# Reordering the first group of batches of an attention kernel: norms in a row, a later bias addition, alternating PSUM banks

## The chip, the cores and the metric

The kernel runs on one core of a Trainium2 chip. A time is the device time of one whole execution in microseconds (us). All executions told of here are of the state "fast" (the usual, undisturbed one) unless said otherwise. A ratio is the mean time of one kernel's fast runs over the mean of the other's fast runs of the same rounds on the same chip, so it is not quite the ratio of the medians that I quote. An interval behind a ratio is its 95% interval.

Engines in the profile: PE is TensorE's matmul stream, PEld its weight load, DVE VectorE, ACT ScalarE, POOL GpSimd, SP SyncE. "PEclk" is the granted TensorE clock as a share of full speed. A pass is one matmul record of the profile; a float32 product shows as two (the adjacency product of one batch is x2 at L306 of the kernel before), a transpose as one (four are x4 at L299). PSUM is the memory of the tiles that the kernel's matmuls write; a bank is one half of its two-bank tiles.

## The reference

128 batches `x[b]` of 128 x 512 float32 go through two pre-norm layers. Cut to what matters:

```python
h = max(layernorm(x), 0)
C = adj @ h + b;  x = x + max_over_nodes(relu(C))    # one number per row (A - A cancels)
# layer 1
h = max(layernorm(x), 0)
q, k, v = h @ Wq + bq, h @ Wk + bk, h @ Wv + bv       # 8 heads of 64
w = softmax(q k^T / 8 + mask(adj == 0))
out = x + w v
```

The first layer adds one number to a whole row, and the second norm takes a row's mean away, so one norm serves both. The weights of a softmax sum to 1, so `bv` may be added to `x` itself, once, at any time before the output. That freedom is what the change uses.

## The kernel before

Batches are worked in groups of four. The first two groups and two batches of the third are prepared by a hand-written beginning; then a loop over 128 batches takes a batch's scores, mask, weighted sum and output, and in the gaps the projections of the next group and the norm of the batch ten ahead. The parts that matter:

```python
def norm_end(m):
    nc.vector.tensor_scalar(HN[m], X[g][:, i, :], MV[m][:, 0:1], 0.0, op0=ALU.subtract, op1=ALU.max)
    nc.scalar.activation(HN[m], HN[m], AF.Copy, scale=RSTD[m])
    nc.gpsimd.tensor_tensor(X[g][:, i, :], X[g][:, i, :], bv_sb, op=ALU.add)
# norm(m), before it: statistics on VectorE, rstd on GpSimd (a power)

def transposes(m):                       # "Tm" in what follows
    ph = ps_sc.tile([P, 2, NC, D], F32, name="sc")       # pool of one two-bank tile
    for c in range(NC):
        nc.tensor.transpose(ph[:, 0, c], HN[m][:, c * P : (c + 1) * P], ident)
    nc.scalar.copy(HT[g][:, i], ph[:, 0])

def adjacency(m, pa=None):               # "Am"
    nc.tensor.matmul(pa, adjT, HN[m], start=True, stop=True)
    nc.vector.reduce_max(AMAX[g][:, i : i + 1], pa, axis=AX.X)

for m in range(G):
    norm(m); norm_end(m)
    if m > 0:
        early(m - 1)                     # early(m): transposes(m), adjacency(m)
plain_q(0)                               # 2 banks, each written and read by halves
early(G - 1)
...                                      # k and v products of group 0, early(4) ... A9
# ---- the loop, at its end:
    if m < B:
        adjacency(m)
    finish(g, i, w)                      # weighted sum, output
```

## Time and profile before

| | before |
|---|---|
| median (range), 3 runs | 1621.87 us (1621.35 to 1623.84) |
| span of the profiled execution | 1620.0 us |
| TensorE busy | 98% |
| first scores of the loop | 75.04 us |
| batch 124's scores, where the last group begins | 1594.57 us |
| from there to the end of the flag (the last VectorE instruction), "the tail" | 22.63 us |
| from there to the end of the span, "the exit" | 2.79 us |

I split the span at three marks, because TensorE bounds most of it: the first scores, the scores of batch 124 (the first of the last four, after which no projections are left to fill the gaps), and the flag that the kernel computes last. The marks are read from the chain of waits; the timeline has the same scores start 0.06 to 0.07 us earlier.

The tail in the kernel before, from the timeline (start, duration, engine, line, what, and the idle time before):

```profile
1600.54 1.16 PE L477 MATMUL sc<-qT,kT 64*128 64x128 f32 x16
1603.22 0.34 PE L499 MATMUL pav<-v,w 128*64 128x65 f32 x4 [1.52 <-DVE w L490]
...
1604.70 1.16 PE L477 MATMUL sc<-qT,kT 64*128 64x128 f32 x16
```

The reader sees a period of 4.16 us: scores, 1.5 us of waiting for the mask, the weighted sum, scores again. TensorE idles here, because nothing is left to put in.

### The profile page before, as it was taken

The page shows a single profiled execution, that of the slowest core. Times are in us where ns is not written, and L with a number is a line of the kernel's source. Part 1 is how long each engine was busy: PE and PEld are TensorE (multiplying, and loading weights), DVE is VectorE, ACT ScalarE, POOL GpSimd, SP SyncE. Part 2 cuts the span into 40 slices and gives each one's busy share as a digit, 9 for nine tenths or more (in the row PEclk, how much of TensorE's full clock was granted, in tenths as well). Part 3 has the DMA queues.
Part 4 walks back from the last instruction along what each step waited for, and adds up shares of the span by engine and source line. Part 5 has one row for each costly group of instructions (what it writes and reads, how often), then busy time and mean ns, then how long its engine had stood idle before and what let it go on. Part 6 is the DMA issues. An engine that isn't in the chain of part 4 may idle for free.

```text
span 1620.0 us, 29469 instructions
## 1 busy us (share of the span) xinstructions
PE 1586.6 (98%) x11819; PEld 1319.8 (81%) x11819; DVE 1114.2 (69%) x2044; ACT 422.9 (26%) x844; POOL 259.6 (16%) x278
## 2 busy tenths in 40 slices
PE   6899999999999999999999999999999999999996
PEld 4688888888888888888888888888888888888885
DVE  3576777766777767777767777667777677777655
ACT  2322222222222222222222222222222222222221
POOL 4311111111111111111111111111111111111000
PEclk9999999999999999999999999999999999999999
DMA  4033222232222232222332222322222322223201
GB/s 164 1 72 73 68 60 51 69 75 69 63 46 70 69 79 65 67 44 69 72 73 68 54 56 69 76 68 64 47 69 69 79 65 67 44 69 73 47 27 40
DMA packets 299082, 104.02 MB, mean 64 GB/s; under 512 B 264448, under 2 KB 264576, under 8 KB 298944
## 3 DMA queue, kind: packets, MB, share of 16 engines
q1 hardware_dynamic: 297520, 99.69, 25.5%
q8 instruction: 94, 1.54, 0.4%
q10 hardware_dynamic: 1248, 2.16, 0.4%
q14 instruction: 44, 0.36, 0.1%
q0 software_dynamic: 176, 0.27, 0.1%
HBM read 37.03 MB, written 33.55 MB: 44 GB/s over the span
## 4 chain that ended last, share of the span: by engine, by line
PE 97%; DVE 1%; ACT 1%; issue 0%; DMA 0%; POOL 0%; ACTq 0%; DVEq 0%; POOLq 0%
PE mm L372 72%; PE pav L499 9%; PE sc L477 8%; PE mm L306 6%; PE mm L445 1%; PE pav L306 1%; PE sc L299 0%; DVE w L490 0%; DMA xg<-in_x_dram 0%; ACT hn L272 0%; DVE o L512 0%; DVE o L508 0%; POOL rstd L264 0%; DVE st L259 0%; ACT qT L450 0%
## 5 line engine op out<-in xcount | busy, mean ns | idle before, releaser
L264 POOL TENSOR_TENSOR rstd<-ve,mhalf 128x1 f32<-128x1 f32 x128 | 84.3, 659 | 1225.9 <-DVE ve L262 1087.6
L485 ACT ACTIVATE w<-sc 128x512 f32<-128x512 f32 x256 | 138.9, 595 | 515.4 <-PE sc L477 515.4
L499 PEld LDWEIGHTS pav<-v,w 128*64 128x64 f32 x4096 | 130.3, 137 | 99.6 <-issue 54.4
L372 PE MATMUL mm<-hs,sq_sb 128*128 128x256 f32 x744 | 179.0, 383 | 0.0
L372 PE MATMUL mm<-hs,sk_sb 128*128 128x256 f32 x768 | 176.4, 379 | 0.0
L372 PE MATMUL mm<-sv_sb,hs 128*128 128x256 f32 x768 | 176.2, 379 | 0.0
L273 POOL TENSOR_TENSOR xg<-xg,bv_sb 128x512 f32<-128x512 f32 x128 | 162.9, 1273 | 35.2 <-DVE hn L269 27.5
L490 DVE TENSOR_TENSOR w<-w,live 128x512 f32<-128x512 f32 x256 | 164.7, 685 | 1.0 <-ACT w L485 1.0
L372 PEld LDWEIGHTS mm<-sv_sb,hs 128*128 128x128 f32 x768 | 145.9, 190 | 20.7 <-issue 1.0
L272 ACT ACTIVATE hn<-hn,rstd 128x512 f32<-128x512 f32 x128 | 92.9, 726 | 267.7 <-DVE hn L269 206.3
L372 PEld LDWEIGHTS mm<-hs,sk_sb 128*128 128x128 f32 x768 | 145.9, 190 | 20.3 <-issue 0.5
L372 PEld LDWEIGHTS mm<-hs,sq_sb 128*128 128x128 f32 x744 | 138.8, 190 | 21.4
L499 PE MATMUL pav<-v,w 128*64 128x65 f32 x4096 | 148.5, 224 | 6.7 <-DVE w L490 6.7
L477 PE MATMUL sc<-qT,kT 64*128 64x128 f32 x2048 | 148.7, 285 | 0.0
L420 DVE TENSOR_TENSOR u<-mm,p1b 128x512 f32<-128x512 f32 x63 | 43.5, 691 | 128.3 <-PE mm L372 128.3
L477 PEld LDWEIGHTS sc<-qT,kT 64*128 64x128 f32 x2048 | 124.2, 187 | 9.1 <-issue 0.3
L372 PE MATMUL mm<-hT,wk_sb 128*128 128x256 f32 x512 | 124.2, 385 | 0.0
L372 PE MATMUL mm<-wv_sb,hT 128*128 128x256 f32 x512 | 120.9, 379 | 0.0
L306 PE MATMUL mm<-hn,adjT 128*128 128x512 f32 x236 | 120.5, 592 | 0.0
L372 PE MATMUL mm<-hT,wq_sb 128*128 128x256 f32 x496 | 120.4, 386 | 0.0
L372 PEld LDWEIGHTS mm<-wv_sb,hT 128*128 128x128 f32 x512 | 97.3, 190 | 13.7 <-issue 0.5
L372 PEld LDWEIGHTS mm<-hT,wk_sb 128*128 128x128 f32 x512 | 94.7, 190 | 15.8 <-issue 0.5
(84 smaller groups left out, 2033.1 us busy)
## 6 DMA issues: line engine op xcount, KB each, us to landing
out_dram<-o SPq DMA_DIRECT2D x128, 256.0 KB, 2.1
xg<-in_x_dram SPq DMA_DIRECT2D x62, 512.0 KB, 5.1
hT<-tb SPq DMA_DIRECT2D x960, 32.0 KB, 2.0
xg<-in_x_dram SPq DMA_DIRECT2D x2, 256.0 KB, 3.4
xg<-in_x_dram ACTq DMA_DIRECT2D x2, 256.0 KB, 5.6
wq_sb<-in_L_gnn_Wq_dram SPq DMA_DIRECT2D x1, 512.0 KB, 7.9
wk_sb<-in_L_gnn_Wk_dram SPq DMA_DIRECT2D x1, 512.0 KB, 11.1
wq_sb<-in_L_gnn_Wq_dram ACTq DMA_DIRECT2D x1, 512.0 KB, 10.6
```

The lines of the kernel that those rows point to most:

```text
L264: nc.gpsimd.tensor_tensor(rstd, ve, mhalf, op=ALU.pow)
L272: nc.scalar.activation(HN[m], HN[m], AF.Copy, scale=RSTD[m])
L273: nc.gpsimd.tensor_tensor(X[g][:, i, :], X[g][:, i, :], bv_sb, op=ALU.add)
L306: nc.tensor.matmul(pa, adjT, HN[m], start=True, stop=True)
L372: nc.tensor.matmul(bank[:, r, :], lhs, rhs, start=first and r == 0 and c == 0, stop=r == 1 and c == 1, skip_group_check=True,)
L420: nc.vector.tensor_tensor(self.u3, self.b, self.pf[1], op=ALU.add)
L445: nc.tensor.matmul(bank[:, r, :], W["q"][:, c, k * P : (k + 1) * P], h[:, :, c], start=r == 0 and c == 0, stop=r == 1 and c == NC - 1, ski ...
L477: nc.tensor.matmul(psc[:, j, f, :], KT[g][r, f, i * D : (i + 1) * D], QT[g][r, f, i * D : (i + 1) * D], start=True, stop=True,)
L485: nc.scalar.activation(w[:, j], psc[:, j], AF.Exp, scale=HD ** -0.5)
L490: nc.vector.tensor_tensor(w[:, j], w[:, j], live_h, op=ALU.mult)
L499: nc.tensor.matmul(pav[r, h // 4, (h % 4) * HE : (h % 4 + 1) * HE], w[:, h % 2, h // 2, r], V[g % 2][:, i, h, :], start=True, stop=True,)
```

## The change

Its intent: start TensorE earlier and leave fewer holes before the first scores. Four parts: (1) all four norms of the first group in a row, with four buffers; (2) the `bv` additions of these four moved to the loop; (3) transposes and adjacency products in the two halves (banks) of one PSUM tile in turn, and `plain_q` by whole banks, with adjacency products between; (4) the norm of a later batch begun right after the adjacency product of the one before. Besides these, ScalarE's activation table is loaded early by a dummy instruction (the load takes 1.28 us in both kernels, from 5.58 us before and from 5.65 us after), and some sums move. The core:

```diff
+        nc.gpsimd.memset(mhalf, -0.5)
+        nc.scalar.activation(live[:, 0:1], mhalf, AF.Copy)
         make_identity(nc, ident)
@@ norm_end
-            nc.gpsimd.tensor_tensor(X[g][:, i, :], X[g][:, i, :], bv_sb, op=ALU.add)
+            if m >= G:
+                add_bv(m)
@@ transposes (adjacency likewise, with ps_av)
-            ph = ps_sc.tile([P, 2, NC, D], F32, name="sc")
+            if i % 2 == 0:
+                PH[g] = ps_sc.tile([P, 2, NC, D], F32, name="sc")
+            ph = PH[g][:, i % 2]
@@ the beginning
             for m in range(G):
                 norm(m)
                 norm_end(m)
-                if m > 0:
-                    early(m - 1)
-            plain_q(0)
-            early(G - 1)
+            transposes(0)
+            transposes(1)
+            plain_q(0, 0)
+            for m in (2, 3):
+                transposes(m)
+            for m in (0, 1):
+                adjacency(m)
+            plain_q(0, 1)
+            for m in (2, 3):
+                adjacency(m)
 ... (sums and norms of the second group: cut)
-                if s >= 8 and s < 12:
-                    h_sum(1, s - 8)
+                if s in (7, 8, 9, 10):
+                    h_sum(1, s - 7)
@@ the loop
                 w = scores(g, i)
+                if g == 0:
+                    add_bv(b)
```

More of the change, by code (lines that the diff above doesn't have):

```diff
@@ L208, in fast @@
         ps_av = ctx.enter_context(tc.tile_pool(name="ps_av", bufs=1, space=PSUM))
-        X, HN, TB, HT, HB, QT, KT, C, AMAX, WA, RSTD, MV, PR = ({} for _ in range(13))
+        X, HN, TB, HT, HB, QT, KT, C, AMAX, WA, RSTD, MV, PR, PH, PA = ({} for _ in range(15))
         def load(g):
@@ L235, in fast @@
         load(2)
+        nc.gpsimd.memset(mhalf, -0.5)
+        nc.scalar.activation(live[:, 0:1], mhalf, AF.Copy)
         make_identity(nc, ident)
-        nc.gpsimd.memset(mhalf, -0.5)
         nc.gpsimd.memset(ones, 1.0)
@@ L245, in fast @@
         nc.scalar.copy(adjT, pt[:, :D])
-        nc.vector.tensor_single_scalar(live, adjT, 0.0, op=ALU.not_equal)
         live_h = live.unsqueeze(1).to_broadcast([P, NC, D])
@@ L255, in norm @@
                 C[g] = stat.tile([P, G], F32, name="c")
-            HN[m] = proj.tile([P, N], F32, name="hn")
+            if m in (2, 3):
+                if m == 2:
+                    TB[0] = proj.tile([P, NQ, 2, NC, Q], F32, name="tb")
+                HN[m] = TB[0].rearrange("p a i c r -> p (a i c r)")[:, (m - 2) * N : (m - 1) * N]
+            else:
+                HN[m] = proj.tile([P, N], F32, name="hn")
             st = stat.tile([P, 6], F32, name="st")
@@ L272, in norm_end, with add_bv @@
             nc.scalar.activation(HN[m], HN[m], AF.Copy, scale=RSTD[m])
-            nc.gpsimd.tensor_tensor(X[g][:, i, :], X[g][:, i, :], bv_sb, op=ALU.add)
+            if m >= G:
+                add_bv(m)
+        def add_bv(m):
+            x_m = X[m // G][:, m % G, :]
+            nc.gpsimd.tensor_tensor(x_m, x_m, bv_sb, op=ALU.add)
         def blocks(m):
@@ L296, in transposes, with adjacency @@
             g, i = divmod(m, G)
-            ph = ps_sc.tile([P, 2, NC, D], F32, name="sc")
+            if i % 2 == 0:
+                PH[g] = ps_sc.tile([P, 2, NC, D], F32, name="sc")
+            ph = PH[g][:, i % 2]
             for c in range(NC):
-                nc.tensor.transpose(ph[:, 0, c], HN[m][:, c * P : (c + 1) * P], ident)
-            nc.scalar.copy(HT[g][:, i], ph[:, 0])
-        def adjacency(m, pa=None):
+                nc.tensor.transpose(ph[:, c], HN[m][:, c * P : (c + 1) * P], ident)
+            nc.scalar.copy(HT[g][:, i], ph)
+        def adjacency(m):
             g, i = divmod(m, G)
-            if pa is None:
+            if m >= 2 * G + 2:
                 pa = ps_mm.tile([P, 512], F32, name="mm")
+            else:
+                if i % 2 == 0:
+                    PA[g] = ps_av.tile([P, 2, 512], F32, name="pav")
+                pa = PA[g][:, i % 2]
             nc.tensor.matmul(pa, adjT, HN[m], start=True, stop=True)
@@ L433, in p3, with plain_q @@
                 self.add(self.dst(0, 1), self.c, self.u2)
-        def plain_q(t):
-            if t == 0:
+        def plain_q(t, f):
+            if t == 0 and f == 0:
                 QT[0] = proj.tile([P, NC, T], F32, name="qT")
             h = HT[0][:, 2 * t : 2 * t + 2]
-            for f in range(2):
-                bank = ps_mm.tile([P, 2, HT2], F32, name="mm")
-                for r in range(2):
-                    k = 2 * f + r
-                    for c in range(NC):
-                        nc.tensor.matmul(
-                            bank[:, r, :], W["q"][:, c, k * P : (k + 1) * P], h[:, :, c],
-                            start=r == 0 and c == 0, stop=r == 1 and c == NC - 1,
-                            skip_group_check=True,
-                        )
-                    nc.scalar.activation(
-                        QT[0][:, k, t * HT2 : (t + 1) * HT2], bank[:, r], AF.Identity,
-                        bias=bq_sb[:, k : k + 1],
-                    )
+            bank = ps_mm.tile([P, 2, HT2], F32, name="mm")
+            for r in range(2):
+                for c in range(NC):
+                    nc.tensor.matmul(
+                        bank[:, r, :], W["q"][:, c, (2 * f + r) * P : (2 * f + r + 1) * P],
+                        h[:, :, c], start=r == 0 and c == 0, stop=r == 1 and c == NC - 1,
+                        skip_group_check=True,
+                    )
+            for r in range(2):
+                k = 2 * f + r
+                nc.scalar.activation(
+                    QT[0][:, k, t * HT2 : (t + 1) * HT2], bank[:, r], AF.Identity,
+                    bias=bq_sb[:, k : k + 1],
+                )
         def products(g):
@@ L517, in fast @@
         with tc.manual_schedule():
-            def early(m):
-                transposes(m)
-                adjacency(m, ps_av.tile([P, 2, 512], F32, name="pav")[:, 0])
             for m in range(G):
@@ L526, in fast @@
                 norm_end(m)
-                if m > 0:
-                    early(m - 1)
-            plain_q(0)
-            early(G - 1)
+            nc.vector.tensor_single_scalar(live, adjT, 0.0, op=ALU.not_equal)
+            transposes(0)
[8 more added lines that the diff above has]
+                adjacency(m)
             weight_sums(nc.vector, "k")
+            plain_q(1, 0)
+            weight_sums(nc.gpsimd, "v")
             for k in range(4):
                 h_sum(0, k)
-            plain_q(1)
-            weight_sums(nc.gpsimd, "v")
+            norm(G)
+            norm_end(G)
+            plain_q(1, 1)
             _, k, v = PR[0] = [None] + [Products(0, n) for n in "kv"]
+            m = G
             for s, p in enumerate((
@@ L540, in fast @@
                 p()
-                m = G + s // 2
-                if m < 2 * G + 2:
-                    if s % 2 == 0:
+                if s % 2 == 0 and m < 2 * G + 2:
+                    if m < 2 * G:
+                        transposes(m)
+                    else:
+                        blocks(m)
+                    adjacency(m)
+                    m += 1
+                    if m < 2 * G + 2:
                         norm(m)
                         norm_end(m)
-                    elif m < 2 * G:
-                        early(m)
-                    else:
-                        blocks(m)
-                        adjacency(m, ps_av.tile([P, 2, 512], F32, name="pav")[:, 0])
-                if s >= 4 and s % 2 == 0 and s < 12:
-                    weight_sum(nc.gpsimd, "q", s // 2 - 2)
-                if s >= 8 and s < 12:
-                    h_sum(1, s - 8)
+                if s in (2, 4, 6, 9):
+                    weight_sum(nc.gpsimd, "q", (2, 4, 6, 9).index(s))
+                if s in (7, 8, 9, 10):
+                    h_sum(1, s - 7)
             move(2 * G + 1)
```

## The prediction

> **What bounds the kernel now.** I read the page first, then the busy table by stretches, the chain of waits for the first 130 us, the timeline of that stretch, and the transfers' landing times.
>
> ```profile
> span 1620.0 us, 29469 instructions
> PE 1586.6 (98%) x11819; PEld 1319.8 (81%) x11819; DVE 1114.2 (69%) x2044; ACT 422.9 (26%) x844; POOL 259.6 (16%) x278
> PE   6899999999999999999999999999999999999996
> ```
>
> TensorE is busy 98% of the span. One digit of the last line is 40.5 us: only the first two or three slices and the last leave it idle, so the span is one TensorE stream of fixed length, and a change of the beginning can only move its start and the holes before it becomes solid. The stretches show the holes (columns: TensorE, weight load, VectorE, ScalarE, GpSimd):
>
> ```profile
> 10.00:15.00 5.00, 0.47 (x1) 0.00 (x0) 3.08 (x5) 0.91 (x2) 2.89 (x3) 1.00 1.05 386
> 15.00:20.00 5.00, 4.66 (x12) 2.74 (x13) 1.73 (x5) 1.53 (x3) 2.07 (x4) 1.00 1.05 387
> ...
> 50.00:55.00 5.00, 3.31 (x17) 2.59 (x17) 2.62 (x6) 0.77 (x2) 2.21 (x3) 1.00 0.00 0
> ```
>
> From 75.04 us, where the chain reaches the first scores, it holds nothing but TensorE through 130 us. So I ask only when the first scores start. The timeline tells why TensorE stands still from 10.5 to 15.3 us (columns: start, duration, engine, line, what):
>
> ```profile
> 12.11 1.26 POOL L273 TENSOR_TENSOR xg<-xg,bv_sb 128x512 f32<-128x512 f32 x1 [6.42 <-DVE mv L260]
> 12.12 1.53 DVE L269 TENSOR_SCALAR hn<-xg,mv 128x512 f32<-128x512 f32 x1
> 13.33 0.73 POOL L264 TENSOR_TENSOR rstd<-ve,mhalf 128x1 f32<-128x1 f32 x1
> ...
> 14.09 0.72 ACT L272 ACTIVATE hn<-hn,rstd 128x512 f32<-128x512 f32 x1 [6.35 <-POOL rstd L264]
> 14.72 0.57 ACT L300 COPY hT<-sc 128x512 f32<-128x512 f32 x1
> ...
> 15.34 1.11 PE L299 MATMUL sc<-ident,hn 128*128 128x128 f32 x4 [4.87 <-ACT hT L300]
> ```
>
> The 6.42 us before GpSimd's addition are put down to VectorE, which had long been done. The bv load, issued at 3.5 us, took 8.5 us to land by the table of transfers: 12.0 us. [...]the first batch's bv addition holds up the second batch's rstd (whose input was ready at 6.3 us), and so on through scaling, ScalarE's copy and the second transposes. Later holes:
>
> ```profile
> 22.51 3.72 PE L445 MATMUL mm<-hT,wq_sb 128*128 128x256 f32 x16 [0.56 <-ACT qT L450]
> ...
> 54.26 0.66 PE L299 MATMUL sc<-ident,hn 128*128 128x128 f32 x4 [1.69 <-ACT hn L272]
> ...
> 65.92 1.13 PE L306 MATMUL pav<-hn,adjT 128*128 128x512 f32 x2 [1.76 <-ACT hn L272]
> ...
> 72.19 1.12 PE L306 MATMUL pav<-hn,adjT 128*128 128x512 f32 x2 [1.69 <-ACT hn L272]
> ```
>
> Here the norm is begun only after the previous adjacency's maximum, with two projection products too few beside it; and inside the plain q projection half a bank waits four times for ScalarE to read the other half.
>
> [...]a pass of the adjacency product takes 0.86 us up to 18 us and 0.43 us at 29 us; the switch lies near 19.4 us, 4.1 us after work resumes at 15.34. [...]1.53 us above beside the bv addition, 0.48 us otherwise. [...]
>
> **The change part by part.** No arithmetic is removed; TensorE's matmuls are the same. I write Tm, Am for transposes and adjacency of batch m.
>
> *Table load.* ScalarE's own DMA issues run to 5.49 us (the last waits for x of batch 1), and before, the load started at 5.58. Worth 0.1 us, eaten by the dummy activation: 0.
>
> *Four norms in a row.* rstd of batch 1 is free at 7.1 us instead of 14.06. Batch 3's x is last: issued at 1.65, 7.3 us to landing (the median of that queue's two is 5.6, the first took 3.9), so about 8.95. From the trace's norm: statistics to rstd's end 1.9 us (3.77 to 5.70), so 10.9; scaling 0.7, so 11.6.
>
> *Alternating banks.* I read the waits of the built program, which was not run. T1 waits for ScalarE's copy of T0, T3 for that of T2, A1 for the maximum of A0, A2 of A1, A3 of A2: the guard is kept per tile, and both halves are one tile. So the second bank does not pay. Worse, ScalarE's first copy stands behind all four scalings. Chain: scaling 3 issued 10.93, next ScalarE instruction 0.63 later (as 14.09 to 14.72), copy 0 11.56 to 12.13, T1 12.18 to 13.29 (1.11 at half clock), copy 1 13.33 to 13.90, first q matmul 13.95. Both halves of wq have landed (2.16 plus 10.6 is 12.8).
>
> *TensorE's work from there to the first scores*, full clock, from the chain: 64 q passes and 13 products of 8 passes at 1.74 per 8: 13.9 and 22.6; T2 to T7 at 0.44: 2.6; A0 to A9 at 0.86: 8.6. Sum 47.7.
>
> *Losses after the change* (estimates from the trace's durations): half clock for about 4 us, 2.0. T3 behind copy 2, which stands behind two qT activations (0.84) and takes 0.57: 1.15. A1 and A3 behind a maximum of 0.69 plus 0.2: 0.9 each (A2 has a q half between). For T4 to T7 the chain maximum, statistics, rstd, scaling, measured as 3.5 us from A5's last pass issued (44.08) to the next transposes (47.60), stands beside two products of 3.47: 0.05 each. A8 0.2, A9 0.5, as VectorE has more queued there. Sum 5.9, and 0.7 for what I also cannot assign before (next line): 6.6. First scores: 13.95 + 47.7 + 6.6 = 68.25.
>
> *Check on before:* from T1 at 15.34 the work is 13.9 + 22.6 + 7 × 0.44 + 9 × 0.86 = 47.3; to 75.04 12.4 are lost. Half clock 2.0; four qT waits at 0.54 plus 0.26 of drain, 3.2; T4 0.7, T6 1.84, A8 1.91, A9 1.84, T5 and T7 0.15: 11.6, 0.7 not assigned. The method holds.
>
> Gain 75.04 − 68.25 = 6.8 us: start 15.34 to 13.95 with 0.4 more work left, 1.0; losses 12.4 to 6.6, 5.8. Of these the q order gives 3.2, the norms begun earlier and the maxima about 5.5, against 2.95 of new waits. The four bv additions (1.27 us each, GpSimd 16% busy) run beside the first group's scores: 0. The tail is untouched. 1621.9 − 6.8 = 1615.
>
> **Rivals.** (a) The banks do alternate, if the waits are released by halves: T1 right after scaling 1, q at 12.8, none of the 2.95: 4.1 us more, 1611. For it: the code's intent; against: the waits name those copies and maxima. (b) [...]a q half of 16 passes at 0.43 is 6.9 us, loss up to 3.4 instead of 2.0, and some more of the small holes: 1617. (c) The norms, squeezed just under two products, slip: each T4 to A9 loses 0.5 rather than 0.05, 1617 to 1618. (d) TensorE must run 1586 us anyway and the gain is absorbed by a transfer later: the chain after 75 us has no DMA piece, so I hold it unlikely; 1621.
>
> **Range and chances.** All rivals lie within 11 us of before, while 2% are 32 us. The size of the mis-reckoning I allow is the clock switch (±1.2), the tight norms (+1.5), the waits by tile (−2.9). 1615, 1612 to 1618 for eight in ten; faster by over 2% 0.01, within 98%, slower 0.01.
>
> **What would show it.** In the changed profile: first scores near 68 us; T1 near 12.2 us released by ScalarE's copy, not by the scaling of batch 1; first q matmul near 13.95; passes of 0.43 until about 18 us; no q matmul waiting for a qT activation; A1 and A3 idle near 0.9 after a maximum; T3 idle near 1.1; scaling of batch 3 at 10.9. It is wrong if T1 runs near 8.6 us, if T4 to A9 show holes over 0.5 us, or if the chain after the first scores has pieces that are not TensorE.

## The result, and the profile after

The changed kernel took 1619.07 us in the median (1618.37 to 1621.22, 4 runs), the kernel before 1621.74 us (1621.35 to 1623.84, 4 runs); the ratio is 0.9983 [0.9966, 1.0]. (The fourth run of the kernel before came with this result.) So 2.7 us were gained, not 6.8, and 1619.07 lies above the range of 1612 to 1618. By the interval of the ratio the gain lies anywhere between 0 and 5.5 us, and by the rule of 2% the two kernels are equally fast.

```profile
span 1616.6 us, 29457 instructions
PE 1588.6 (98%) x11819; PEld 1322.9 (82%) x11819; DVE 1115.1 (69%) x2044; ACT 422.6 (26%) x845; POOL 260.7 (16%) x278
```

This is the head of the page after. TensorE executes as many matmuls as before, and is busy 2.0 us longer (1588.6 against 1586.6). The same matmuls took longer: a first hint of the clock.

The busy table of the same stretches as in the prediction (columns: TensorE, weight load, VectorE, ScalarE, GpSimd, granted clock):

```profile
10.00:15.00 5.00, 2.14 (x7) 1.56 (x8) 0.64 (x3) 1.78 (x3) 0.72 (x1) 1.00 1.05 386
15.00:20.00 5.00, 5.00 (x16) 3.98 (x15) 0.00 (x0) 0.00 (x0) 1.11 (x1) 1.00 1.05 387
50.00:55.00 5.00, 5.00 (x26) 3.87 (x25) 3.02 (x7) 1.68 (x3) 3.26 (x5) 1.00 0.00 2
```

The holes of 10 to 15 us and of 50 to 55 us are smaller or gone. The clock column is of no use here: it says 1.00 in the second row, while 16 passes of 256 columns need 5 us. The trace's list of clock stretches begins only at 18.91 us, with the rise to full, and without a record the column shows 1.00. So I read the clock before that from durations. The timeline there:

```profile
10.94 0.72 ACT L277 ACTIVATE tb<-tb,rstd 128x512 f32<-128x512 f32 x1 [1.63 <-POOL rstd L269]
11.57 0.57 ACT L312 COPY hT<-sc 128x512 f32<-128x512 f32 x1
12.19 1.12 PE L311 MATMUL sc<-ident,hn 128*128 128x128 f32 x4 [3.26 <-ACT hT L312]
13.98 6.14 PE L459 MATMUL mm<-hT,wq_sb 128*128 128x256 f32 x16 [0.68 <-ACT hT L312]
19.95 0.60 PE L311 MATMUL sc<-ident,tb 128*128 128x128 f32 x4
21.52 0.66 PE L311 MATMUL sc<-ident,tb 128*128 128x128 f32 x4 [0.97 <-ACT hT L312]
22.02 1.02 PE L322 MATMUL pav<-hn,adjT 128*128 128x512 f32 x2
23.82 1.13 PE L322 MATMUL pav<-hn,adjT 128*128 128x512 f32 x2 [0.78 <-DVE amax L323]
```

T1 (at 12.19) waits for ScalarE's copy of T0, which stands behind the scaling of batch 3 (10.94). The first q half, 16 passes, needs 5.97 us from its start to that of the transposes behind it (19.95 - 13.98; the 6.14 of the line reach 0.17 us into those transposes). At full clock 16 passes take 3.46, twice the 1.73 of eight in the chain of waits. I call this step "the q half" and measure it in this way throughout. T3 (21.52) waits for a copy, A1 (23.82) for a maximum. The last two adjacency products, and the sum on VectorE beside them:

```profile
58.91 1.67 DVE L340 TENSOR_TENSOR hs<-hT 128x512 f32<-128x512 f32 x1
59.60 1.13 PE L322 MATMUL pav<-hn,adjT 128*128 128x512 f32 x2
...
64.21 0.72 ACT L277 ACTIVATE hn<-hn,rstd 128x512 f32<-128x512 f32 x1 [4.66 <-PE mm L388]
...
64.99 1.13 PE L322 MATMUL pav<-hn,adjT 128*128 128x512 f32 x2 [0.81 <-ACT hn L277]
```

First scores: 69.57 us, 5.47 earlier than before. But the span is only 3.4 us shorter. The tail is where the rest is. Its timeline, and below it the busy table:

```profile
1595.07 1.16 PE L493 MATMUL sc<-qT,kT 64*128 64x128 f32 x16
...
1599.22 2.05 PE L493 MATMUL sc<-qT,kT 64*128 64x128 f32 x16
1602.78 2.29 PE L515 MATMUL pav<-v,w 128*64 128x65 f32 x32 [1.51 <-DVE w L506]
1605.00 1.67 PE L493 MATMUL sc<-qT,kT 64*128 64x128 f32 x16
```

```profile
1594.00:1600.00 6.00, 4.21 (x83) 3.78 (x85) 3.55 (x8) 1.09 (x2) 0.00 (x0) 0.94 0.12 46
1600.00:1606.00 6.00, 4.47 (x52) 3.89 (x52) 3.15 (x6) 1.08 (x2) 0.00 (x0) 0.50 0.11 44
```

The second row: granted clock 0.50. The same scores take 2.05 us instead of 1.16. The kernel before had 1.00 in both stretches; its second row:

```profile
1600.00:1606.00 6.00, 4.17 (x86) 3.54 (x81) 3.92 (x8) 1.18 (x3) 0.00 (x0) 1.00 0.12 46
```

The tail took 24.76 us instead of 22.63.

### The profile page after: what moved, and what is told of

Its sections match the earlier page's. It is cut to its first block, busy times and chain, and to the rows that moved or that the text cites. A ratio compares the mean times of both kernels' runs of the same rounds, so it can differ in the third digit from the quotient of the medians.

```text
span 1616.6 us, 29457 instructions
## 1 busy us (share of the span) xinstructions
PE 1588.6 (98%) x11819; PEld 1322.9 (82%) x11819; DVE 1115.1 (69%) x2044; ACT 422.6 (26%) x845; POOL 260.7 (16%) x278
## 3 DMA queue, kind: packets, MB, share of 16 engines
q10 hardware_dynamic: 1248, 2.16, 0.4%
## 4 chain that ended last, share of the span: by engine, by line
PE 98%; DVE 1%; DMA 0%; ACT 0%; issue 0%; POOL 0%; ACTq 0%; DVEq 0%; POOLq 0%
PE mm L388 72%; PE sc L493 9%; PE pav L515 9%; PE mm L322 6%; PE mm L459 1%; PE pav L322 1%; DMA xg<-in_x_dram 0%; DVE w L506 0%; PE sc L311 0%; DVE amax L323 0%; ACT hT L312 0%; DVE o L528 0%; ACT hn L277 0%; DVE o L524 0%; POOL rstd L269 0%
```

## The experiments

Eighteen runs were made on the chip. The marks of each, in us, from its profiled execution:

| kernel | first scores | tail | exit | span | median of its runs | before, same chip |
|---|---|---|---|---|---|---|
| before | 75.04 | 22.63 | 2.79 | 1620.0 | 1621.74 | |
| changed | 69.57 | 24.76 | 2.74 | 1616.6 | 1619.07 | 1621.74 |
| tail_filled | 70.62 | 22.65 | 5.30 | 1618.1 | 1619.72 | 1623.45 |
| shift_13 | 75.33 | 24.29 | 5.45 | 1624.6 | 1626.11 | 1623.45 |
| before_tail_filled | 76.22 | 22.64 | 5.51 | 1623.9 | 1624.95 | 1623.45 |
| start_warmed | 67.82 | 22.63 | 5.52 | 1615.5 | 1617.97 | 1623.45 |
| after_again | 69.52 | 24.78 | 2.77 | 1616.6 | 1618.84 | 1622.90 |
| split_banks | 64.68 | 25.38 | 2.71 | 1612.3 | 1615.10 | 1622.90 |
| bv_in_line | 76.82 | 24.78 | 2.77 | 1623.9 | 1625.79 | 1622.90 |
| before_bv_late | 70.66 | 24.78 | 2.73 | 1617.7 | 1619.90 | 1622.90 |
| fallback_longer | 69.23 | 25.46 | 2.77 | 1617.0 | 1619.63 (one run) | |
| copies_first | 67.14 | 24.75 | 2.78 | 1614.2 | 1616.37 (one run) | |
| tail_lean | 69.62 | 22.63 | 2.72 | 1614.5 | 1617.29 | 1622.86 |
| best_lean | 62.97 | 22.63 | 2.77 | 1607.9 | 1610.05 | 1622.86 |
| before_tail_lean | 73.14 | 22.64 | 2.79 | 1618.1 | 1621.61 | 1622.23 |
| tail_lean_again | 68.90 | 22.63 | 2.74 | 1613.8 | 1616.00 | 1622.23 |
| no_early_table | 69.55 | 25.64 | 2.78 | 1617.5 | 1619.27 | 1622.23 |
| h_sums_later | 69.76 | 22.63 | 2.78 | 1614.7 | 1617.19 | 1622.23 |
| best_lean_again | 63.03 | 22.64 | 2.70 | 1607.9 | 1610.03 | 1623.15 |
| best_both | 62.01 | 22.63 | 2.73 | 1606.9 | 1608.51 | 1623.15 |

All gave correct results. My theory after the result: the beginning went as told except for the clock and A9, and the rest is lost in the tail because TensorE's clock is halved there. The rivals: the tail's loss depends on where in time the tail lies (which the change shifted), or the missing gain went elsewhere.

### The tail

**tail_filled.** The changed kernel, with spare matmuls in the last four batches into a PSUM tile that nobody reads, so that TensorE does not idle while it waits for the mask.

```diff
                 if m < B:
                     adjacency(m)
+                if g + 1 == NG:
+                    fill(3)              # 3 matmuls of 256 columns, never read
                 finish(g, i, w)
```

> The changed kernel with three spare 128x256 matmuls into an unread bank after the scores of each of the last four batches, 1.3 us in a TensorE hole of 1.5 to 1.9 us. Theory (the gain shown at the first scores, 5.48 us, is partly lost again because TensorE falls to half clock in the last four batches, at 1599.2 us in the changed kernel's profile against about 1612 us in that of before): TensorE stays at full clock to the last batch, the tail from the scores of batch 124 (1589.1) to the end shrinks from 27.5 to about 25.4 us, median about 1616.8 to 1617.0 against 1619.1 of the changed kernel, and runs scatter less than 0.5 us. Rival (the tail is slower for another reason: DMA, GpSimd, VectorE): no gain, about 1619, or slower by up to 0.4 us per batch if the spare matmuls hold up the weighted sums.

The tail fell to 22.65 us, with the clock at 1.00 until 1610.97: the clock is the cause of its loss. But the time hardly fell (ratio to before 0.9976 [0.9962, 0.999]), because the exit rose from 2.74 to 5.30 us, and x of batch 3 landed late in this execution (9.64 us instead of 8.98), which put the first scores at 70.62. The longer exit goes with one more packet, 95 instead of 94, on the queue that the page calls "instruction"; in the last 10 us of the span there are two such packets, and one in the kernel before.

**shift_13.** The changed kernel with 13 spare matmuls before the loop, which push its tail to where the tail of the kernel before lies in time.

```diff
+            fill(13)
             move(2 * G + 1)
```

> The changed kernel with 13 spare 128x256 matmuls (5.6 us at full clock) just before the first scores, so that everything after stands where it stood in the kernel before. [...]first scores at 75.2 us, the half clock comes as late in the tail as before (about 1612), span about 1620.2, median about that of before plus 0.2. Rival of a loss that belongs to the changed kernel and not to its place in time: span 1616.6 + 5.6 = 1622.2, median 1624.5.[...]

First scores at 75.33, near those of the kernel before, and the tail still took 24.29 us, with the clock at half from 1609.2 us. So the position in time does not save it, as far as one execution can tell. The median of 1626.11 is not comparable with the expected ones, since an exit of 5.45 us came with the spare matmuls.

**before_tail_filled.** The spare matmuls of tail_filled in the kernel before.

> The kernel before with the same spare matmuls in its last four batches. Theory: its fast runs have the tail at full clock until about 1612 us already, so the median moves by 0 to 0.5 us, but the slow stray run of 1623.84 us should not come back. Rival (the half clock in the tail is the usual state of both kernels): 2 us faster, as much as the changed kernel gains.

The tail is 22.64 us, as it was in the profiled execution of before, the exit 5.51, and the median 1624.95 (ratio 1.0006 [0.9993, 1.002]). That is 1.5 us above the medians of before, where 0 to 0.5 was expected: in the profile the exit is 2.7 us longer and the first scores come 1.2 us later than in before.

**fallback_longer.** To see what makes the exit long: 13 more matmuls in the fallback branch that this input never enters, so that the program is longer but executes nothing more.

```diff
-        nc.tensor.matmul(pa, adjT, hn, start=True, stop=True)
+        for _ in range(14):
+            nc.tensor.matmul(pa, adjT, hn, start=True, stop=True)
```

> The changed kernel with 13 more matmuls in the fallback branch that is never entered, so no executed instruction changes. The four kernels with spare matmuls took 5.3 to 5.5 us from the last flag to the end of the span[...], the others 2.7 to 2.8. Theory[...]: 5.3 to 5.5 us from flag to end here too, span 2.6 us longer for the same first scores and tail, one more instruction packet. Rival (the spare matmuls themselves or that chip did it): 2.7 to 2.8 us.

That expectation fell: the exit was 2.77 us. A longer program in the branch not taken does not lengthen it; the four kernels with 12 to 34 executed spare matmuls had 5.3 to 5.5, those with none to six 2.70 to 2.79. Whether it is their number or where they stand was not tried, and the cause stays open.

**tail_lean.** Fewer spare matmuls: one of 512 and one of 256 columns in each of the last three batches, six in all (two passes each).

```diff
+                if g + 1 == NG and i > 0:
+                    fill(512, 256)
                 finish(g, i, w)
```

> The changed kernel with two spare matmuls (512 and 256 columns, 1.3 us) in each of the last three batches, 6 in all. Theory[...]: from the last group's first scores to the flag 22.6 to 22.7 us instead of 24.8, in all runs; single runs scatter by the clock's rise alone, 1616.5 plus or minus 1 if the end stays at 2.8 us[...]. Rival: 24.8 us or more.

```profile
1594.00:1600.00 6.00, 5.64 (x92) 4.40 (x94) 3.55 (x8) 1.08 (x2) 0.00 (x0) 1.00 0.11 44
1600.00:1606.00 6.00, 5.80 (x64) 3.69 (x62) 4.62 (x9) 2.17 (x4) 0.00 (x0) 1.00 0.13 48
```

TensorE is busy 5.6 to 5.8 of 6 us instead of 4.2 to 4.5, the clock stays at 1.00, the tail takes 22.63 and the exit 2.72 us. Median 1617.29, ratio 0.9963 [0.995, 0.9977]: 1.6 to 1.8 us below the changed kernel's own medians on other chips.

**before_tail_lean and tail_lean_again**, both kernels with the same six spare matmuls on one chip, to see how much of the missing gain is the tail's.

> The kernel before with the six spare matmuls (one of 512 and one of 256 columns in each of the last three batches) that keep the clock up in the tail. Theory (the tail's clock is what hid part of the gain): first scores near 75.0 us as in the kernel before, last batch's scores to the flag 22.63 us, median near 1621.5 us and a scatter below 1 us in place of the up to 5 us of the kernel before on one chip. Rival (the tail of the kernel before is no part of it): scatter and median as the kernel before of the same rounds.

> The changed kernel with the same six spare matmuls, a repeat of an earlier run beside its partner. Theory: first scores near 69.6 us, tail 22.63 us, median near 1617.0 us, so 4.6 to 5.1 us below before_tail_lean (5.47 us gained at the first scores less about 0.4 us outside the span). Rival (the gain is lost elsewhere than in the tail's clock): the difference of the pair stays near 2.7 us, as that of the two kernels themselves.

Medians 1621.61 and 1616.00: a difference of 5.6 us. In the means (1621.73 and 1616.28) it is 5.45, give or take 1.9 (95%, worked out from the scatter of the five runs each), so the 4.6 to 5.1 that I expected fit; the 2.7 us without spare matmuls, give or take 2.1, are lower, but the two overlap. In the two profiles of this pair the first scores lie 4.24 us apart (73.14 and 68.90) and the tails are equal. The expected scatter below 1 us for before_tail_lean was wrong: its five runs go from 1619.82 to 1623.99. Its beginning still plays with the clock: in the three profiles of the beginning of the kernel before (before, before_tail_filled, before_tail_lean) the first scores come at 75.04, 76.22 and 73.14 us. By the list of clock stretches the clock rose at 19.28 us in the first (the prediction read 19.4 from durations). In the second it rose at 11.22, fell at 14.63 and rose again at 21.46; in the third it rose at 12.90, and four transposes at 14.88 us already take 0.66 us.

Over all twenty profiles: of the twelve without spare matmuls in the tail, nine had a tail of 24.3 to 25.6 us and three (before, start_warmed, h_sums_later) 22.63; of the eight with them, none was above 22.65. So the change does not force the loss (start_warmed and h_sums_later contain the whole change), and does not have to be whole for it (before_bv_late). That the kernel before itself suffers it in some executions is likely but not shown: its one profile without spare matmuls was spared until 1613.30 us. That was luck, and I built on it.

What spares a tail that has no spare matmuls is not shown by these traces. In the changed kernel the clock is full from 18.91 to 1599.28 us, and then half for 6.83 us. In the tail, scores and weighted sums with a hole of 1.5 us repeat every 4.16 us. The share of busy TensorE over 6 us (the ends of matmuls are modelled, so it is rough) does not part the spared tail from the other: it was busy 4.21 us in the 6 us from 1594 in the changed kernel, in which the clock fell (at 1599.28), and 4.17 us in the 6 us from 1600 in the kernel before, in which it stayed at 1.00. With the spare matmuls of tail_lean it was busy 5.64 and 5.80 of 6 us, and the clock stayed. These leave the hole of batch 124 as it was in all but the two filled kernels (busy 4.35 us in the 6 us from 1588 in tail_lean_again, at a clock of 1.00), so they are no guarantee; but in all 24 timed executions of tail_lean, best_lean, their repeats and best_both the granted clock is 0.998 or 0.999, while in h_sums_later, without them, it goes from 0.996 to 0.999. No run was made to test how much work keeps the clock up.

### The beginning

**after_again**, the changed kernel once more on another chip, as the partner of the next three.

> The changed kernel once more, unchanged, for more runs on the chip of this group. [...]first scores at 69.0 to 71 us as the clock rises earlier or later, half clock somewhere in or not in the last four batches, single runs spread over 3 us; over more runs the mean gain on the kernel before is nearer the 5.5 us seen at the first scores than the 2.7 us of the first four runs, some 3.5 to 5. Rival (the changed kernel always loses 2 us in the tail): half clock before the last batch again, gain 2.5 to 3.5 us.

First scores 69.52, tail 24.78, ratio 0.9975 [0.9962, 0.9987]. The profile of the changed kernel repeats, with the half clock in the tail, as the rival had it. The gain is 4.1 us in the medians (4.4 in the means), as expected, because 11 runs of the kernel before have a median of 1622.90 here, and the four with the result had 1621.74.

**split_banks.** The two halves of the PSUM tile made two tiles in the first group: the odd batches' transposes and adjacency products go to tiles of another pool.

```diff
             ph = PH[g][:, i % 2]
+            if m in (1, 3):
+                ph = ps_mm.tile([P, 512], F32, name="mm").rearrange("p (c d) -> p c d", c=NC)
@@ adjacency
                 pa = PA[g][:, i % 2]
+                if m in (1, 3):
+                    pa = ps_mm.tile([P, 512], F32, name="mm")
```

> The changed kernel with the odd batches' first transposes and adjacency products in bank tiles of their own. Theory (one tile for two banks keeps the waits): second transposes near 8.7 us instead of 12.2, first q matmul near 12.8 (0.6 later where the loads land later), no waits of 1.0, 0.8 and 0.8 us at T3, A1, A3; first scores near 65.5 us, 4 us earlier than the changed kernel. Rival (VectorE's chain of norms or the landing of wq takes the place of those waits): first scores at 67 to 69 us.

```profile
7.67 1.12 PE L313 MATMUL sc<-ident,hn 128*128 128x128 f32 x4 [2.35 <-ACT hn L277]
8.58 1.06 PE L313 MATMUL mm<-ident,hn 128*128 128x128 f32 x4
12.99 5.52 PE L463 MATMUL mm<-hT,wq_sb 128*128 128x256 f32 x16 [3.35 <-ACT hT L314]
18.34 0.60 PE L313 MATMUL sc<-ident,tb 128*128 128x128 f32 x4
18.78 0.60 PE L313 MATMUL mm<-ident,tb 128*128 128x128 f32 x4
```

T1 follows T0 at once, at 8.58 instead of 12.19, and T3, A1 and A3 no longer wait (A1 starts at 20.07, before the line of A0, 19.21 to 20.23, has ended). First scores 64.68, 4.9 us before the changed kernel's (0.6 of it is the clock: the q half took 5.35 us instead of 5.97); the time is 1615.10 (ratio 0.9951 [0.9939, 0.9963]). So the waits of the change's alternating banks were between parts of one tile, not between banks.

**bv_in_line.** The change without the deferred `bv` (all else as changed; the addition stands in `norm_end` again for all batches).

```diff
-            if m >= G:
-                add_bv(m)
+            add_bv(m)
@@ loop
-                if g == 0:
-                    add_bv(b)
```

> The changed kernel with the bv addition back in each of the first four norms, all else as changed. Theory (the late bv load holds up GpSimd's queue, and the changed order then puts the first copy behind all four scalings): rstd of batch 3 near 17 us instead of 10.2, second transposes near 19 us, first q matmul near 20.8 us, first scores near 76.4, later than the kernel before (75.0); time equal to before or 1 to 2 us slower. Rival (the load of x for batch 3 or wq bounds the start, not bv): first scores within 1 us of the changed kernel's.

First scores 76.82, later than in the kernel before, ratio 1.0013 [0.9998, 1.0027]. GpSimd's first addition starts only at 12.46 us (it needs `bv` from memory), and then GpSimd does additions and rstd of four batches in turn, and ScalarE's first copy, behind all four scalings, comes at 18.37, so T1 starts at 18.99 instead of 15.34. The rest of the change without the deferred addition makes the beginning no better; in time the two kernels do not differ clearly.

**before_bv_late.** The other way about: the kernel before with the deferred `bv` alone.

```diff
-            nc.gpsimd.tensor_tensor(X[g][:, i, :], X[g][:, i, :], bv_sb, op=ALU.add)
+            if m >= G:
+                add_bv(m)
@@ loop, after the scores of batch b
+                if g == 0:
+                    add_bv(b)
```

> The kernel before with only the first four bv additions moved to the first group's scores. Theory (most of the start's gain is the bv load out of the way): second transposes near 10.3 us instead of 15.3, q from about 16.5 instead of 20.2, first scores near 71 us: 4 of the 5.5 us. Rival (the order of norms, transposes and adjacency is what gains): first scores at 74 to 75 us.

```profile
10.36 1.06 PE L304 MATMUL sc<-ident,hn 128*128 128x128 f32 x4
```

T1 starts at 10.36 instead of 15.34 and the first scores come at 70.66, that is 4.4 of the change's 5.5 us. Median 1619.90, ratio 0.9979 [0.9966, 0.9993]: as good as the whole change within the scatter (on this chip 3.0 us below before in the medians, the whole change 4.1). The two profiles differ in their clock too: it rose at 13.24 us here and at 18.91 in the changed kernel, where the q half lost 2.5 us to it. So what the reordering of the rest is worth, 1.1 us at the first scores in these two profiles, is not settled; it loses with T1, T3, A1 and A3 much of what it gains elsewhere.

**start_warmed.** The changed kernel with spare transposes of the identity (12 after the first, 16 after T0, 6 after T1), to raise the clock before the q passes.

```diff
+            warm(12)                      # after the transpose of adj
 ...
             transposes(0)
+            warm(16)
             transposes(1)
+            warm(6)
```

> The changed kernel with spare 128x128 transposes of the identity in TensorE's holes before 13.98 us: 12 before the first transposes, 16 after them, 6 after the second. Theory (the first half of the q projection takes 6.15 us for 16 passes because the clock is still half until 19.4 us[...]): the clock rises before or at 13.98 us, the half takes 3.5 us, first scores 2 to 2.7 us earlier, at about 67 us; in time 2 to 2.7 us less, if the tail does not change with its place. Rival (VectorE's chain behind the first adjacency sets the first scores anyway): the q half is faster but first scores move less than 1 us.

The q half takes 18.18 - 14.62 = 3.56 us instead of 5.97, and the first scores come at 67.82, 1.75 us earlier, though T1 was later here (13.29 against 12.19). The clock rose at 9.16 us here; from 4.84 us until then TensorE did nothing but transposes. Median 1617.97, ratio 0.9968 [0.9955, 0.9982]. The tail was spared in the profile (22.63), but the long exit of 5.52 us takes 2.8 of the 3.9 us that beginning and tail gained.

**copies_first.** The first two transposes and their copies issued before the scalings of batches 2 and 3, so that ScalarE does the copies first.

```diff
             for m in range(G):
                 norm(m)
                 norm_end(m)
+                if m == 1:
+                    transposes(0)
+                    transposes(1)
-            transposes(0)
-            transposes(1)
```

> The changed kernel with the transposes of batches 0 and 1 emitted after their two norms, so that ScalarE copies them before it scales batches 2 and 3; the tiles stay shared. Theory (the first copy stands behind the wait for batch 3's x): second transposes near 9.6 us instead of 12.2, the q half waits only for the second half of wq, about 12.8 to 13.4; first scores near 68.4 to 69.0, 0.6 to 1.2 us earlier. Rival (the copies cost nothing there because wq lands no earlier): within 0.3 us of the changed kernel.

```profile
9.41 1.12 PE L311 MATMUL sc<-ident,hn 128*128 128x128 f32 x4 [0.68 <-ACT hT L312]
11.21 6.46 PE L459 MATMUL mm<-hT,wq_sb 128*128 128x256 f32 x16 [0.68 <-ACT hT L312]
```

The q half starts at 11.21 instead of 13.98, and is done at half clock for still longer (17.50 - 11.21 = 6.29 us). First scores 67.14, 2.4 us earlier and better than expected: the q half did not wait for its weights until 12.8 us or later.

**h_sums_later.** The four sums on VectorE of the second group two products later, away from A9's norm. In the changed kernel's trace the sum of 1.67 us above stands beside GpSimd's addition (58.77 to 60.03 us) and one of 1.76 us, at 64.29, beside the next (64.15 to 65.49), while the one at 63.68, with no addition beside it, takes 0.68. The prediction's 1.53 us against 0.48 are VectorE's subtraction in the norm, beside such an addition (12.11 to 13.37 us) and without.

```diff
-                if s in (7, 8, 9, 10):
-                    h_sum(1, s - 7)
+                if s in (9, 10, 11, 12):
+                    h_sum(1, s - 9)
```

> The changed kernel with the four sums of the second group's activations two products later, so that none stands on VectorE between the norm and the adjacency product of batch 9. Theory (the 0.96 us hole before that adjacency product comes from the sum that VectorE does first, at 1.67 us beside GpSimd's bv addition): hole below 0.3 us, first scores near 68.7 us. Rival (the chain maximum, statistics, rstd, scaling itself is too long by then): hole stays 0.7 to 1.0 us, first scores 69.5 us.

```profile
63.40 1.89 PE L388 MATMUL mm<-sv_sb,hs 128*128 128x256 f32 x8
...
64.41 0.72 ACT L277 ACTIVATE hn<-hn,rstd 128x512 f32<-128x512 f32 x1 [3.75 <-POOL rstd L269]
...
65.18 1.12 PE L322 MATMUL pav<-hn,adjT 128*128 128x512 f32 x2
```

The product of 8 passes that starts at 63.40 ends 1.73 us later (the step from one product to the next), so A9's hole is 65.18 - 65.13 = 0.05 us; in the changed kernel it was 64.99 - (62.29 + 1.73) = 0.97. The first scores stand at 69.76, because x of batch 3 landed later here and T1 started at 13.03. To compare kernels in spite of this, take the start of T1 and the q half away: 69.57 - 12.19 - 5.97 = 51.41 in the changed kernel, 68.90 - 12.49 - 4.99 = 51.42 in tail_lean_again, 69.55 - 12.99 - 5.14 = 51.42 in no_early_table. In h_sums_later it is 69.76 - 13.03 - 6.24 = 50.49. So this edit is worth 0.9 us, as expected, though its expected first scores of 68.7 were missed.

### Outside the span

The time of an execution less its span is 1.8 us in the kernel before (means of 1.76 to 1.82 on five chips) and 2.1 in the changed kernel and its relatives with the early table load (means of 2.08 to 2.16 where they were timed in rounds; the one run of fallback_longer has 2.63, which nothing here explains).

**no_early_table.** The changed kernel with the table load where it was.

```diff
-        nc.gpsimd.memset(mhalf, -0.5)
-        nc.scalar.activation(live[:, 0:1], mhalf, AF.Copy)
         make_identity(nc, ident)
+        nc.gpsimd.memset(mhalf, -0.5)
```

> The changed kernel without the moved memset and dummy activation (the activation table is loaded where it was before). Theory (the 0.4 us that the changed kernel takes outside the profile's span come from the early table load[...]): time less span of the profiled execution 1.7 to 1.8 us as in the kernel before, the start of the first transposes and the first scores as in the changed kernel within 0.2 us, median about 0.4 us lower at the same tail. Rival (the 0.4 us come from elsewhere, or the table load matters to the beginning): time less span stays 2.1 to 2.2 us, or the first scores come later by more than 0.5 us.

Time less span is 1.77 us in the profiled run and 1.86 in the mean of five. The first scores stay at 69.55. The versions of the kernel before, which have no early table load either, have 1.75 to 1.82. So the early table load gains nothing and costs 0.3 us which the profile does not show. How it does that is open. The median of 1619.27 is no judge of 0.3 us: the tail was long here (25.64 us).

### The versions that beat both

**best_lean.** split_banks, copies_first, three spare matmuls of 512 columns to raise the clock in the beginning and three in the tail, and `bv` deferred for the first ten batches.

> The changed kernel with odd batches' first transposes and adjacency products in tiles of their own, copies of batches 0 and 1 before the scalings of 2 and 3, bv added later for the first ten batches, one spare 512-column matmul before the first transposes and two after the second, one in each of the last three batches. Theory: clock up before the first q matmul, q half 3.5 us, first q matmul at 12.8 to 13.4, no waits at T3, A1, A3, hole before A9 under 0.5 us: first scores at 61 to 63 us; the tail may fall to half clock still, as one spare matmul fills only half of the hole; time 1610 to 1613. Rival (VectorE's chain of norms sets the pace once the waits are gone): first scores near 64 us, no better than the kernel with split tiles.

Median 1610.05 (1609.54 to 1610.29), ratio 0.992 [0.9906, 0.9933]. With the clock kept up at both ends (the q half took 16.63 - 12.87 = 3.76 us, the tail 22.63) the scatter of five runs is 0.75 us (1.19 in best_lean_again).

**best_lean_again and best_both.** best_lean once more, and best_lean with the edits of h_sums_later and no_early_table, on one chip.

> A repeat of the kernel with split banks, early copies, warm start, later bv and three spare matmuls in the tail, beside the next run. Expected: first scores near 63.0 us, tail 22.63 us, time less span 2.1 us, median near 1610 us with a scatter below 1 us.

> The same kernel with the sums of the second group's activations two products later and without the moved table load. Theory (both terms are real and independent of the clock): hole before the adjacency product of batch 9 from 0.8 to near 0.05 us, first scores near 62.1 us, time less span 1.8 us in place of 2.1, median 1.0 to 1.3 us below best_lean_again. Rival (they were side effects of the clock or of the chip): median within 0.3 us of best_lean_again.

```profile
55.65 1.89 PE L405 MATMUL mm<-sv_sb,hs 128*128 128x256 f32 x8
...
57.43 1.12 PE L339 MATMUL pav<-hn,adjT 128*128 128x512 f32 x2
```

A9's hole is 57.43 - 55.65 - 1.73 = 0.05 us, the first scores come at 62.01 instead of 63.03, time less span is 1.8 to 1.9 instead of 2.05 to 2.2, and the medians are 1608.51 and 1610.03: 1.5 us (1.36 in the means). That is a little above the 1.0 to 1.3 expected, so the two terms add, as far as the scatter lets one see. best_both is the best kernel here, at a ratio of 0.9906 [0.989, 0.9921] to the kernel before.

## Why the prediction was wrong

**What held.** The start by its own steps: scaling of batch 3 at 10.93 predicted, 10.94 measured; T1 at 12.18 and 12.19; first q matmul 13.95 and 13.98; T3's stall 1.15 and 1.13 (21.52 less 19.95 and the 0.44 of T2); no q matmul waits for a qT activation. Reading the waits of the built program was right: they are kept per tile, and split_banks shows it by a run. The stretch from the first scores to those of batch 124 took 1519.53 us in both, so nothing was given back there, as rival (d) had it. Of the rivals: (a) was refused for the change as built, and is what split_banks makes of it (4.9 us at the first scores, 4.3 without the clock's part, against the 4.1 told); (b) happened in part, with a loss of 2.5 us in place of 2.0 or 3.4; (c) happened for A9 alone.

**What was mis-sized.** "Half clock for about 4 us, 2.0": the q half took 5.97 us instead of 3.46, so 2.5. start_warmed nearly removes the loss, with 3.56. "A8 0.2, A9 0.5": the holes were 0.30 (59.60 less 57.57, where the product before it starts, and 1.73) and 0.97, so 1.27 in place of 0.7, because a sum on VectorE took 1.67 us beside GpSimd's addition and stood before A9's norm; h_sums_later takes away 0.9. Together 1.1 of the 1.32 us by which the first scores (69.57) missed 68.25; the rest is small change in the holes before T4 to T7, A1 and A3.

**What failed.** "The tail is untouched. 1621.9 − 6.8 = 1615." The instructions of the tail are untouched, but they do not alone fix the clock at which they run. The tail took 24.76 us instead of 22.63, 2.13 more, with TensorE at half clock from 1599.28 to 1606.11; tail_lean, with work in the holes, has 22.63 again. The prediction took the tail of one profile as fixed, and it was a lucky one. With the clock kept up in the tail of both kernels the change is worth 5.45 us in the means, give or take 1.9 (before_tail_lean and tail_lean_again). A smaller step that failed: "*Table load.* ... 0": it costs 0.3 us outside the span (no_early_table, best_both).

The sum for the profiled run of the changed kernel, timed 1618.8: 1615.0, and 1.32 at the first scores, 2.13 in the tail and 0.3 outside the span, make 1618.75. That this agrees to 0.05 is partly luck: in this one execution 0.48 us, not 0.3, were lost outside the span (2.20 against 1.72), and the base is a median of three runs. The range failed for the same reason: it allowed for the clock's switch in the beginning only (±1.2), and had no term for the end.

**What stays open.** What decides in an execution whether the tail is spared is open, and so is why all ten timed runs of the changed kernel were hit (their granted clocks, 0.994 to 0.997, suggest it; the changed beginning does not force it, by start_warmed and h_sums_later). How often the kernel before is hit I cannot say: on five chips its granted clock was 0.998 or more in 21 of 47 executions, with spans of 1619.4 to 1620.7, and 0.992 to 0.997 in the others, with spans of 1619.5 to 1624.6. This mean counts the clock only from its first rise (the profile of before has 0.998 with 6.7 us at half after it), and a clock that falls again in the beginning, as in before_tail_filled, lowers it too; I have no profile of one of the long ones, and do not know how its loss divides between beginning and tail. Also open are how a table load costs time outside the span, and why 12 and more spare matmuls lengthen the exit.

## What to carry to other kernels

Where TensorE bounds a kernel, look at both ends for stretches in which it idles (it was busy 4.2 of 6 us in the tail here): the clock there was a lottery of 2 us and more in this kernel (tails of 22.63 or 24.3 to 25.6), and three to six spare matmuls into an unread PSUM tile kept it up in every profile; with 12 the exit grew by more than the tail gained (2.6 against 2.1 us in tail_filled). Two halves of one tile are no double buffer when waits are kept per tile: make two tiles (4.9 us at the first scores in split_banks), and read the waits of the built program. And before reordering much, ask which single instruction holds up an engine's next ones (in the kernel before, GpSimd's first `bv` addition at 12.11 us kept the second rstd, its input ready at 6.3 us, until 13.33): moving the `bv` addition off GpSimd's first norms alone gave 4.4 of 5.5 us at the first scores (with some help of an earlier clock), and 3.0 of 4.1 us in the medians.
